# Four stacked graph-attention layers on one core: lighter VectorE work in the one-head layer, and the last layer's dense product turned round

## The chip, the cores and the metric

One core of a Trainium2 chip runs the whole program. The metric is device time in microseconds (us) of one launch; the time before is the median of three runs. A profiled execution of the same program gives the trace from which durations are read.

## The reference

Four graph-attention layers, each `x = x + gat(relu(layernorm(x)), adj)`, over 3327 nodes with 512 features in float32. The graph is sparse: a node has about 17 neighbours on average, itself among them. In each layer (heads 8, 4, 1, 8; head width 512 / heads):

```
h   = features @ W                                  # [n, heads, d]
e   = leaky_relu(s1[:, None] + s2[None, :], 0.2)    # s1, s2: one number per node and head
e   = where(adj > 0, e, -inf)
out = softmax(e, over neighbours) @ h               # layers 1 and 2 then take elu(out)
```

The slope is 0.2. A factor of `exp` that depends on the target node alone drops out of the softmax, which the kernel uses throughout.

## The kernel before

**Two ways to reach neighbours.** Nodes are sorted by neighbour count and cut into 26 tiles of 128 (`NT`), the fullest first. A tile's neighbours are listed in up to `CAPS[t]` slots per node (36, 25, 23, 22, ... 11). Most tiles go *by lists*: for each slot an indirect DMA, issued by POOL, gathers 128 rows of 528 floats (features and scores) from a table in DRAM. The first tiles are taken *dense* instead: 0, 1, 9 and 3 of them in layers 0 to 3 (`DENSE`). For these the 26 source tiles are walked in order, with a byte mask of who is whose neighbour.

**Steps.** A list tile works in groups of four slots. One group is a *step*: layer 2 (one head) has 72 steps, layer 3 (the last) has 105. A loop over steps writes the instructions of PE, DVE, ACT and POOL in an order fixed by hand. Within step `s` the order is: gathers for the step four ahead (`fetch`, five buffers, `LOOK = 5`; a list tile's own rows come by a DMA that SP issues), pieces placed "first", the next group's scores (`scored`), pieces placed "scored", this group's sums (`group`), pieces placed "last". Every other piece (dense work, ends of tiles) is put into this order with `later(s, place, piece)`. Each engine runs its instructions in this order and waits on semaphores.

**List groups.** `scored`: two DVE instructions form `z` (L888 adds target and source score, L890 is the leaky relu), ACT takes the exponential (L891); at a tile's first group DVE first copies the target's score out of the gathered row (L886). `group` with more than one head: DVE multiplies each gathered row by its weights (L919, `m`), PE adds the products into a PSUM bank with an identity matrix (L924, `bank<-m,ident`). With one head DVE does both in one instruction per slot (L912).

**End of a tile.** DVE divides by the sum of weights; then, except in the last layer, layer norm, four transposes (L451) and the 16-matmul projection to the next layer's table (L469).

**Dense tiles of layer 2 (`Wholes`).** Nine tiles in three passes of three. For source tile `j`: ACT makes the weights `r` of 128 sources x 384 targets in PSUM (`weights`, L1128), DVE adds `c` and applies the mask (`masked`, L1135, into `em`), PE multiplies (`products`, L1162, three matmuls 128 x 512). The sum of weights per target is built on the way: POOL adds `em` in pairs (`paired`, L1148), DVE adds two pairs and the running sum in a strided reduction (`added`, L1154), and at the end of a pass three small matmuls with a column of ones sum over partitions (`divisors`, L1169). `Whole.means` divides on DVE (L1089).

**Dense tiles of layers 1 and 3 (`Several`).** In layer 3, three tiles at once, in two passes of four heads. A *unit* is one source tile in one pass; there are 52. Per unit: two loads by SP (feature columns and mask, L1259 and L1260, three buffers each); ACT makes the weights of four heads (`weights`, L1276, 128 x 384 each) in three PSUM banks `r` and scales the features by `c` into `vs` (`features`, L1287, two buffers); one DVE instruction of 128 x 1536 masks all four heads (`masked`, L1292, into `e`, two buffers); and PE runs twelve matmuls (`products`, L1310), for each of three target tiles and four heads, with the 128 x 128 weights stationary and the head's 65 feature columns moving, each column run given twice, so 130 columns. Unit `u` stands in step `u * (steps - 8) / 52`; its products come one step later.

On this chip a float32 matmul shows as two records of the matmul and two of its weight load, so 624 of these matmuls are 1248 records.

Of the kernel before, what the change touches and what calls it, by code (L numbers as in the profile page):

```python
# [380 lines left out]
class Weights:  # L381
# [19 lines left out]
    def fold(self):  # L401

        if not self.left:
            return
        nc, HF = self.nc, self.HF
        s, k = self.left.pop(0)
        prod = self.work.tile([P, 2 * HF], F32, name="prod", bufs=1)
        nc.vector.tensor_mul(prod.rearrange("p (s n) -> p s n", s=2), self.w[:, k, :, :HF],
                             self.av[:, s, :].rearrange("p (s n) -> p s n", s=2))
        nc.vector.tensor_reduce(self.w[:, k, s, HF:HF + self.H],  # L410
                                prod.rearrange("p (h d) -> p h d", d=self.D), AX.X, OP.add)


# [383 lines left out]
def tile_gat_lists(ctx: ExitStack, tc: tile.TileContext, x, adj, ws, avs, out, ident, half, slots, L, low, spare, tabx, tabs):  # L797
# [48 lines left out]
    class Tile:  # L846
# [29 lines left out]
        def scored(self, i):  # L876

            H = HEADS[self.l]
            t = self.t
            k0, n, g = self.groups[i]  # L880
            if i == 0:
                self.po = pools["o"].tile([P, BANK], F32, name="bank")
                pw = next(scores)
                K = CAPS[t]
                self.wt, self.s = pw[:, :K * 8].rearrange("p (k h) -> p k h", h=8), pw[:, K * 8:K * 8 + H]
                nc.vector.tensor_copy(self.s, g[:, n, F:F + H] if self.l == 0 else g[:, 0, F // 2:F // 2 + H])  # L886
            z = small.tile([P, GROUP, 8], F32, name="z")[:, :n, :H]
            nc.vector.tensor_tensor(z, g[:, :n, ROW - 8:ROW - 8 + H],  # L888
                                    self.s.unsqueeze(1).to_broadcast([P, n, H]), OP.add)
            nc.vector.scalar_tensor_tensor(z, z, SLOPE, z, OP.mult, OP.max)  # L890
            nc.scalar.activation(self.wt[:, k0:k0 + n, :H], z, AF.Exp)  # L891
            if self.l == 0:
                ranks = n - (i == 0)
                nc.scalar.activation(slots(t, max(k0, 1), count=ranks), g[:, :ranks, F // 2], AF.Copy)
                if i == 0:
                    nc.scalar.activation(xs[self.t], g[:, n, :F], AF.Copy)
# [187 lines left out]
    class Whole(Tile):  # L1084


        def means(self):
            self.y = low[:, self.t % 3 * F:(self.t % 3 + 1) * F]
            nc.vector.tensor_scalar(self.y, self.po, self.den, None, OP.mult)  # L1089

    class Wholes:


        def __init__(self, l, W):
# [6 lines left out]
            self.a = [low[:, 5 * F + p % 2 * wide:5 * F + (p % 2 + 1) * wide] for p in range(ND // 3)]  # L1101
            self.v, self.e, self.mk, self.r, self.pairs, self.parts = {}, {}, {}, {}, {}, {}

# [14 lines left out]
        def weights(self, p, j):  # L1118
# [3 lines left out]
            if p == 0:  # L1122
# [3 lines left out]
                nc.scalar.activation(mc, c, AF.Copy, scale=-1.0)  # L1126
            r = self.r[p, j] = pools["o"].tile([P, wide], F32, name="r")
            nc.scalar.activation(r, self.a[p], AF.Relu, scale=b, bias=mc)  # L1128

        def masked(self, p, j):  # L1130

            if j % 2 == 0:
                self.two = pools["e"].tile([P, 2, wide], F32, name="em", bufs=3)
            self.e[p, j] = self.two[:, j % 2, :]
            nc.vector.scalar_tensor_tensor(self.e[p, j], self.r.pop((p, j)), self.c[:, j:j + 1],  # L1135
                                           self.mk.pop((p, j)), OP.add, OP.mult)
            if j % 2:
                self.pairs[p, j // 2] = self.two

        def part(self, p, i):  # L1140
            if (p, i) not in self.parts:
                self.parts[p, i] = pools["e"].tile([P, 3, wide], F32, name="parts", bufs=2)
            return self.parts[p, i]

        def paired(self, p, i):

            two = self.pairs.pop((p, i))
            nc.gpsimd.tensor_tensor(self.part(p, i // 2)[:, 1 + i % 2, :], two[:, 0, :], two[:, 1, :], OP.add)  # L1148

        def added(self, p, i):  # L1150

            parts = self.part(p, i // 2)[:, i < 2:2 + i % 2, :]
            out_ = self.a[p] if i == NT // 2 - 1 else self.part(p, i // 2 + 1)[:, 0, :]
            nc.vector.tensor_reduce(out_, parts.rearrange("p j c -> p c j"), AX.X, OP.add)  # L1154

# [9 lines left out]

        def divisors(self, p):
            self.pd = pools["t"].tile([P, F // P, P], F32, name="pt")
            for q in range(3):
                nc.tensor.matmul(self.pd[:, 0, q:q + 1], self.a[p][:, q * P:(q + 1) * P], one, start=True, stop=True)  # L1169

        def means(self, p):
            den = small.tile([P, 3], F32, name="den3")
            nc.vector.reciprocal(den, self.pd[:, 0, :3])
            for q in range(3):
                tl = self.tiles[3 * p + q]
                tl.den = den[:, q:q + 1]
                tl.means()

        def place(self, n):

            per = n // (ND // 3)
            for p in range(ND // 3):
                s0 = p * per
                later(s0 - 4 if p else -1, "first", lambda p=p: self.targets(p))
                for j in range(NT):
# [7 lines left out]
                    if j % 2:  # L1193
                        i = j // 2
                        later(s + 1, "first", lambda p=p, i=i: self.paired(p, i))
                        if i % 2 or j == NT - 1:
                            later(s + 2, "last", lambda p=p, i=i: self.added(p, i))
                later(s + 3, "first", lambda p=p: self.divisors(p))
                later(s + 3, "last", lambda p=p: self.means(p))
# [15 lines left out]
    class Several:  # L1215
# [3 lines left out]
        def __init__(self, l, n, W):  # L1219
# [11 lines left out]

            self.vs = [room((Q + (self.H == 8)) * DV) for _ in range(2)]
            self.v = [room(ROW // 2) for _ in range(3)]
            self.mk = [room(n * P // 4).bitcast(U8) for _ in range(3)]
            self.s = room(n * 8).rearrange("p (t h) -> p t h", h=8)
            for t in range(n):
                nc.sync.dma_start(self.s[:, t, :self.H],
                                  tabs[l % 2][t * P:(t + 1) * P, F // 2:F // 2 + self.H])
            self.per = BANK // DV - (self.H == 8)

        def begin(self):

            if self.H == 8:
                for vs in self.vs:
                    nc.scalar.activation(vs[:, self.Q * self.DV:], ident[:, :self.DV], AF.Copy, scale=0.0)
            for q in range(self.n):
# [48 lines left out]
        def products(self, u):  # L1295
# [8 lines left out]
            for q in range(self.n):  # L1304
                for h in range(Q):
                    o, o0 = self.where(q, h)
                    dst, mov = o[:, o0:o0 + DV], vs[:, h * DV:(h + 1) * DV]
                    if self.H == 8:
                        dst, mov = twice(dst, self.per * DV - o0), twice(mov, (Q - h) * DV)
                    nc.tensor.matmul(dst, e[:, h, q * P:(q + 1) * P], mov, start=False, stop=(j == NT - 1),  # L1310
                                     skip_group_check=True)

# [20 lines left out]
        def place(self, s0, s1):  # L1333
# [12 lines left out]
            for q in range(self.n):  # L1346
                self.tiles[q].ends(s + 1 + 2 * q)

    at = {}

# [10 lines left out]
    for l in range(NL):  # L1361
# [3 lines left out]
        with ExitStack() as c2:  # L1365
# [13 lines left out]
            else:  # L1379
                pools.update(m=pool("mpool", 5))  # L1380
                pools.update(p=pool("ps_p", 1 if DENSE[l] else 2, **psum))
                if DENSE[l]:
                    pools.update(w=pool("ps_w", l // 3 + 1, **psum), r=pool("ps_r", 1, **psum))
                    if DENSE[l] > 1:
                        pools.update(e=pool("epool", 1))
                    wholes = Several(l, DENSE[l], W)
                    pw = pools["p"].tile([P, BANK], F32, name="pw")
# [21 lines left out]
            elif DENSE[l]:  # L1409
                wholes.place(0, len(steps) - 8)  # L1410
            at_end = len(steps) + 30
# [69 lines left out]
```

## Time and profile before

| what | value |
|---|---|
| median of three runs | 2940.11 us (2933.88 to 2944.69) |
| profiled execution | 2959.5 us |
| its span, first to last instruction | 2957.8 us |
| mean granted TensorE clock | 0.867 |
| busy over the span | PE 75%, DVE 65%, POOL 58%, ACT 32% |
| DMA | 594.20 MB, 201 GB/s over the span |
| layer 2 in the trace | about 1856 to 2293 us |
| layer 3 in the trace | about 2300 to 2958 us |

The profile gives one execution. Busy time is the time in which an engine had an instruction running; a line such as L1310 names the kernel line. PE is the matmul, PEld its weight load. "Idle before, releaser" is how long an engine stood still ahead of these instructions and whose signal ended it; "issue" means that no signal is seen for which it waited.

### The profile page before, as it was taken

The page shows a single profiled execution, that of the slowest core. Times are in us where ns is not written, and L with a number is a line of the kernel's source. Part 1 is how long each engine was busy: PE and PEld are TensorE (multiplying, and loading weights), DVE is VectorE, ACT ScalarE, POOL GpSimd, SP SyncE. Part 2 cuts the span into 40 slices and gives each one's busy share as a digit, 9 for nine tenths or more (in the row PEclk, how much of TensorE's full clock was granted, in tenths as well). Part 3 has the DMA queues.
Part 4 walks back from the last instruction along what each step waited for, and adds up shares of the span by engine and source line. Part 5 has one row for each costly group of instructions (what it writes and reads, how often), then busy time and mean ns, then how long its engine had stood idle before and what let it go on. Part 6 is the DMA issues. An engine that isn't in the chain of part 4 may idle for free.

```text
span 2957.8 us, 27080 instructions
## 1 busy us (share of the span) xinstructions
PE 2224.7 (75%) x7082; PEld 1251.4 (42%) x7082; DVE 1914.3 (65%) x4968; ACT 931.8 (32%) x2502; POOL 1728.5 (58%) x1717
## 2 busy tenths in 40 slices
PE   4777677787677745788877787689696778877887
PEld 2664243343333323344434344245354445444453
DVE  7887656565546523767765565698887556666665
ACT  5882122222221101323332222344333333333330
POOL 7894465565556663555655552676764555555554
PEclk9988788888888877899988889799897889988898
DMA  6885477677666675666766663788775666666664
GB/s 229 322 294 160 140 218 216 193 235 222 188 205 195 189 194 170 181 202 192 209 193 189 192 192 111 226 264 257 236 248 152 191 177 184 185 182 194 185 187 137
DMA packets 260730, 594.20 MB, mean 201 GB/s; under 512 B 103699, under 2 KB 121107, under 8 KB 256214
## 3 DMA queue, kind: packets, MB, share of 16 engines
q0 software_dynamic: 124368, 432.13, 49.8%
q1 hardware_dynamic: 132454, 153.45, 16.5%
q10 hardware_dynamic: 3744, 6.82, 0.7%
q8 instruction: 57, 0.93, 0.1%
q14 instruction: 107, 0.88, 0.1%
HBM read 542.60 MB, written 49.65 MB: 200 GB/s over the span
## 4 chain that ended last, share of the span: by engine, by line
DVE 21%; PE 18%; issue 16%; another core or an unknown queue 11%; ACT 6%; POOL 4%; DMA 3%; DVEq 0%; ACTq 0%; POOLq 0%; SPq 0%
PE bank L924 11%; DVE m L919 9%; POOL g L835 3%; PE pv L469 3%; PE whole L1310 3%; DVE bank L912 2%; DMA g<-tab,idxb 1%; DVE z L890 1%; DVE z L888 1%; ACT r L1276 1%; DVE x L962 1%; DVE q L439 1%; ACT pw L891 1%; DVE room L1292 1%
## 5 line engine op out<-in xcount | busy, mean ns | idle before, releaser
L924 PE MATMUL bank<-m,ident 128*128 128x512 f32 x2414 | 1236.5, 659 | 268.9 <-DVE m L919 137.5
L835 POOL DMA_INDIRECT g<-tab,idxb x712 | 678.2, 952 | 465.5 <-issue 189.3
L919 DVE TENSOR_TENSOR m<-g,pw 128x512 f32<-128x512 f32 x1207 | 752.0, 682 | 267.6 <-ACT pw L891 193.5
L924 PEld LDWEIGHTS bank<-m,ident 128*128 128x128 f32 x2414 | 490.2, 211 | 879.8 <-issue 568.9
L469 PE MATMUL pv<-w,hT 128*128 128x264 f32 x1664 | 447.4, 423 | 107.0 <-ACT hT L458 71.2
L835 POOL DMA_INDIRECT g<-tabx,twiceb x342 | 324.1, 948 | 245.8 <-issue 124.4
L835 POOL DMA_INDIRECT g<-tab,idxa x297 | 283.1, 953 | 262.1 <-DMA tab<-v 88.5
L469 PEld LDWEIGHTS pv<-w,hT 128*128 128x128 f32 x1664 | 339.5, 208 | 215.2 <-ACT hT L458 79.6
L891 ACT ACTIVATE pw<-z 128x32 f32<-128x32 f32 (+4 forms) x356 | 67.8, 190 | 945.4 <-DVE z L890 509.8
L1162 PE MATMUL whole<-ve,em 128*128 128x512 f32 x468 | 224.5, 632 | 48.2 <-DVE em L1135 27.9
L1310 PE MATMUL whole<-L,room 128*128 128x130 f32 x1248 | 171.1, 288 | 79.2 <-issue 79.0
L1310 PEld LDWEIGHTS whole<-L,room 128*128 128x128 f32 x1248 | 163.1, 201 | 107.1 <-issue 104.7
L695 POOL TENSOR_TENSOR key<-a,keys 128x3328 int32<-128x3328 int32 (+1 forms) x29 | 189.5, 6539 | 15.9 <-DVE cand L704 12.6
L912 DVE SCALAR_TENSOR_TENSOR bank<-g,L,bank 128x512 f32<-128x512 f32 x243 | 183.3, 754 | 9.9 <-remote 2.0
L835 POOL DMA_INDIRECT g<-tabx,twicea x99 | 94.4, 954 | 119.6 <-issue 75.3
L1162 PEld LDWEIGHTS whole<-ve,em 128*128 128x128 f32 x468 | 92.8, 203 | 158.7 <-issue 114.6
L451 PE MATMUL pt<-ident,xn 128*128 128x128 f32 x416 | 74.5, 302 | 93.0 <-issue 32.2
L704 DVE MAX8 cand<-key 128x8 f32<-128x208 int32 x416 | 143.6, 363 | 0.1
L890 DVE SCALAR_TENSOR_TENSOR z<-z 128x32 f32<-128x32 f32 (+5 forms) x428 | 82.5, 193 | 91.4 <-remote 61.4
L919 DVE TENSOR_TENSOR bank<-g,pw 128x512 f32<-128x512 f32 x74 | 51.5, 696 | 126.7 <-ACT pw L891 105.6
L1276 ACT ACTIVATE r<-low,L 128x384 f32<-128x384 f32 x208 | 121.2, 582 | 9.8 <-remote 3.9
L888 DVE TENSOR_TENSOR z<-g,pw 128x32 f32<-128x32 f32 (+4 forms) x356 | 61.8, 174 | 94.9 <-DMA g<-tab,idxa 39.0
(181 smaller groups left out, 2154.4 us busy)
## 6 DMA issues: line engine op xcount, KB each, us to landing
a<-in_adj SPq DMA_DIRECT2D x25, 1664.0 KB
tab<-v SPq DMA_DIRECT2D x78, 264.0 KB
ve<-tab SPq DMA_DIRECT2D x78, 264.0 KB
g<-tab SPq DMA_DIRECT2D x65, 264.0 KB
tabx<-vx SPq DMA_DIRECT2D x26, 528.0 KB
g<-tab,idxb POOLq DMA_INDIRECT x712
low<-tab SPq DMA_DIRECT2D x52, 132.0 KB
spare<-tab SPq DMA_DIRECT2D x52, 132.0 KB
```

The costliest lines, as they stand in the source:

```text
L469: nc.tensor.matmul(pv[:, s, :HF + 8], hT[:, k, :], W.w[:, k, s, :], start=(k == 0), stop=(k == KC - 1))
L695: nc.gpsimd.tensor_tensor(key[:, c:c + quarter], a[:, c:c + quarter], keys[:, c:c + quarter], OP.mult)
L704: nc.vector.max(cand[:, g * 8:(g + 1) * 8], key[:, g * SEG:(g + 1) * SEG])
L835: nc.gpsimd.indirect_dma_start(out=out_, out_offset=None, in_=table, in_offset=bass.IndirectOffsetOnAxis(ap=which, axis=0))
L890: nc.vector.scalar_tensor_tensor(z, z, SLOPE, z, OP.mult, OP.max)
L891: nc.scalar.activation(self.wt[:, k0:k0 + n, :H], z, AF.Exp)
L912: nc.vector.scalar_tensor_tensor(acc, v, w, acc, OP.mult, OP.add)
L919: nc.vector.tensor_tensor(out_.rearrange("p (s h d) -> p s h d", s=2, d=D), v.rearrange("p s (h d) -> p s h d", d=D), wt[:, k0 + q, :H].re ...
L924: nc.tensor.matmul(self.po, ident, m[:, q, :], start=False, stop=(k0 + q == K - 1), skip_group_check=True)
L1162: nc.tensor.matmul(tl.po.rearrange("p (s m) -> p s m", s=2), e[:, q * P:(q + 1) * P], v.rearrange("p (s m) -> p s m", s=2)[:, :, :F // 2], ...
L1276: nc.scalar.activation(self.r[:, h, :], self.a[:, g, :], AF.Relu, bias=-1.0, scale=self.b[:, j, g:g + 1])
L1310: nc.tensor.matmul(dst, e[:, h, q * P:(q + 1) * P], mov, start=False, stop=(j == NT - 1), skip_group_check=True)
```

## The change

In the one-head layer, the table of features carries two more columns: 0.8 times the target's score and 0.2 times the source's. The score `z` becomes `max(s2 + 0.8 s1, 0.2 s2)`, one DVE instruction, and ACT copies the target's score. `Whole.means` goes to ACT. The weights `r` get one PSUM bank for the whole layer, and the sums of weights go into columns of the same bank: POOL's pair sums are summed over partitions by PE, three matmuls of one column for each pair of source tiles, in place of the DVE reductions.

In the last layer `Turned` takes the place of `Several`: four passes of two heads, 104 units. The 65 feature columns of a head are stationary, and its weights for all three target tiles (384 columns) move: two matmuls per unit. Results stand transposed, so each pass ends with copies out of PSUM, 24 PE transposes in all for the four passes, and the division. Per unit the mask is 128 x 768, `vs` has three buffers, `e` two, and each unit has its own load of mask and features. Units are spread over half steps ("first" and "last"), with three steps between passes. Layer 1 keeps `Several`, whose eight-head branches go.

```diff
@@ Weights.fold
+        if self.H == 1:
+            nc.vector.tensor_scalar(self.w[:, k, s, HF + 1:HF + 2], self.w[:, k, s, HF:HF + 1],
+                                    SLOPE if s else 1.0 - SLOPE, None, OP.mult)
@@ Tile.scored
-                nc.vector.tensor_copy(self.s, g[:, n, F:F + H] if self.l == 0 else g[:, 0, F // 2:F // 2 + H])
+                if H == 1:
+                    nc.scalar.activation(self.s, g[:, 0, F // 2 + 1:F // 2 + 2], AF.Copy)
+                else:
+                    nc.vector.tensor_copy(self.s, g[:, n, F:F + H] if self.l == 0 else g[:, 0, F // 2:F // 2 + H])
             z = small.tile([P, GROUP, 8], F32, name="z")[:, :n, :H]
+            if H == 1:
+                nc.vector.scalar_tensor_tensor(z, g[:, :n, ROW - 8:ROW - 7], self.s, g[:, :n, ROW - 7:ROW - 6],
+                                               OP.add, OP.max)
+                nc.scalar.activation(self.wt[:, k0:k0 + n, :H], z, AF.Exp)
+                return
@@ Whole.means
-            nc.vector.tensor_scalar(self.y, self.po, self.den, None, OP.mult)
+            nc.scalar.activation(self.y, self.po, AF.Copy, scale=self.den)
@@ Wholes
+            bank = pools["o"].tile([P, BANK], F32, name="r")
+            self.r, self.pd = bank[:, :wide], [bank[:, wide + 8 * p:wide + 8 * p + 3] for p in range(ND // 3)]
...
         def paired(self, p, i):
             two = self.pairs.pop((p, i))
-            nc.gpsimd.tensor_tensor(self.part(p, i // 2)[:, 1 + i % 2, :], two[:, 0, :], two[:, 1, :], OP.add)
+            self.sums[p, i] = pools["e"].tile([P, wide], F32, name="sums", bufs=3)
+            nc.gpsimd.tensor_tensor(self.sums[p, i], two[:, 0, :], two[:, 1, :], OP.add)
         def added(self, p, i):
-            parts = self.part(p, i // 2)[:, i < 2:2 + i % 2, :]
-            out_ = self.a[p] if i == NT // 2 - 1 else self.part(p, i // 2 + 1)[:, 0, :]
-            nc.vector.tensor_reduce(out_, parts.rearrange("p j c -> p c j"), AX.X, OP.add)
+            both = self.sums.pop((p, i))
+            for q in range(3):
+                nc.tensor.matmul(self.pd[p][:, q:q + 1], both[:, q * P:(q + 1) * P], one, start=(i == 0 and q == 0),
+                                 stop=(i == NT // 2 - 1), skip_group_check=True)
...
-                        if i % 2 or j == NT - 1:
-                            later(s + 2, "last", lambda p=p, i=i: self.added(p, i))
-                later(s + 3, "first", lambda p=p: self.divisors(p))
+                        later(s + 3, "first", lambda p=p, i=i: self.added(p, i))
@@ Turned (new; takes Several's place in layer 3)
+        def features(self, u):
...
+            for h in range(Q):
+                nc.scalar.activation(vs[:, h, :D], self.v[u % 3][:, h * D:(h + 1) * D], AF.Copy,
+                                     scale=self.c[:, j, h0 + h:h0 + h + 1])
+            nc.scalar.activation(vs[:, :, D], self.c[:, j, h0:h0 + Q], AF.Copy)
+        def masked(self, u):
+            n = self.n * P
+            nc.vector.scalar_tensor_tensor(self.e[u % 2], self.r, 1.0,
+                                           self.mk[u % 3].unsqueeze(1).to_broadcast([P, self.Q, n]), OP.add, OP.mult)
+        def products(self, u):
+            j, e, vs, DV = u % NT, self.e[u % 2], self.vs[u % 3], self.DV
...
+            for h, o in enumerate(self.po):
+                nc.tensor.matmul(o[:DV, :self.n * P], vs[:, h * DV:(h + 1) * DV], e[:, h, :], start=(j == 0),
+                                 stop=(j == NT - 1))
...
+        def turned(self):
...
+                    nc.tensor.transpose(self.pt[:, q, h, :], self.sums[:DV, h, q * P:(q + 1) * P], ident[:DV, :DV])
...
+            halves = 2 * (s1 - s0 - 3 * (self.passes - 1))
+            for u in range(self.passes * NT):
+                i, j = divmod(u, NT)
+                s, b = divmod(2 * (s0 + 3 * i) + u * halves // (self.passes * NT), 2)
+                place = "last" if b else "first"
+                later(s, place, lambda u=u: self.masked(u))
+                later(s, "last" if b else "scored",
+                      lambda u=u: (self.weights(u + 1), self.features(u + 1), self.load(u + 3)))
+                later(s + 1, place, lambda u=u: self.products(u))
+                if j == NT - 1:
+                    later(s + 2, "scored", self.summed)
+                    later(s + 3, "first", self.turned)
+                    later(s + 3, "last", lambda i=i: self.means(i))
@@ tile_gat_lists
-                wholes.place(0, len(steps) - 8)
+                wholes.place(0, len(steps) - (10 if many else 8))
```

## The prediction

> **What bounds the kernel now.** First the busy time by stage: the window view over layer 2's dense part and over layer 3 (columns: window, length, busy time and records of PE, PEld, DVE, ACT, POOL, granted clock, DMA share, GB/s).
>
> ```profile
> 1856.00:2230.00 374.00, 308.29 (x891) 168.32 (x892) 313.75 (x630) 146.53 (x361) 257.48 (x273) 0.91 0.80 244
> 2300.00:2950.00 650.00, 521.34 (x2001) 308.45 (x2000) 408.39 (x800) 202.66 (x629) 362.66 (x382) 0.89 0.64 183
> ```
>
> Layer 2: DVE 84%, PE 82%, POOL 69%. But each gather is followed by 0.30 us of issue, so POOL's 215 gathers in this window hold it 215 x (0.97 + 0.30) = 273 us, with pair sums (38) and roots (13) 324: three engines close to full. Layer 3: PE 80%, DVE 63%, POOL with 383 x 0.30 of issue about 478 of 650.
>
> Next, what DVE does in these stages that the change touches (groups by line and form: busy us, mean ns | idle before). The first four lines are of 1856 to 2293 us, the last two of the whole page:
>
> ```profile
> L1154 DVE TENSOR_REDUCE parts<-parts 128x384 f32<-128x1152 f32 x15 | 22.0, 1467 | 0.0
> L890 DVE SCALAR_TENSOR_TENSOR z<-z 128x4 f32<-128x4 f32 x58 | 14.2, 245 | 4.3 <-DVE z L888 2.4
> L1089 DVE TENSOR_SCALAR low<-whole,den 128x512 f32<-128x512 f32 x9 | 6.2, 744 | 0.1
> L1135 DVE SCALAR_TENSOR_TENSOR em<-r,c,mk 128x384 f32<-128x384 f32 x78 | 47.8, 612 | 24.8 <-issue 10.1 <-ACT r L1128 8.5 <-ACT hT L458 4.8
> ...
> L924 PE MATMUL bank<-m,ident 128*128 128x512 f32 x2414 | 1236.5, 659 | 268.9 <-DVE m L919 137.5
> L1310 PE MATMUL whole<-L,room 128*128 128x130 f32 x1248 | 171.1, 288 | 79.2 <-issue 79.0
> ```
>
> The last line is odd: 79 us of idle ahead of products that wait for no signal. The timeline shows what it is. These lines are from one spot of layer 3 (start, length, engine, instruction, idle before):
>
> ```profile
> 2415.71 2.17 PE L1310 MATMUL whole<-L,room 128*128 128x130 f32 x18
> ...
> 2418.78 0.27 PE L1310 MATMUL whole<-L,room 128*128 128x130 f32 x1 [0.89 <-issue]
> ...
> 2420.18 0.19 PEld L1310 LDWEIGHTS whole<-L,room 128*128 128x128 f32 x1 [2.37 <-issue]
> 2420.84 0.94 POOL L835 DMA_INDIRECT g<-tab,idxa  x1 [0.30 <-issue]
> 2421.59 0.38 PE L1310 MATMUL whole<-L,room 128*128 128x130 f32 x1 [2.54 <-issue]
> ...
> 2425.85 0.95 POOL L835 DMA_INDIRECT g<-tab,idxa  x1 [0.30 <-issue]
> 2426.50 0.38 PE L1310 MATMUL whole<-L,room 128*128 128x130 f32 x1 [1.75 <-issue]
> ...
> 2430.30 1.06 ACT L1287 ACTIVATE L<-spare,low 128x64 f32<-128x64 f32 x4 [8.51 <-remote]
> ...
> 2431.57 2.48 DVE L919 TENSOR_TENSOR m<-g,pw 128x512 f32<-128x512 f32 x4 [9.54 <-ACT pw L891]
> ```
>
> PE runs 18 of this unit's 24 product records in 2.17 us; the last six take 12 us, one instruction per 0.7 or 1.4 us. ACT waits for them (it may not overwrite `vs`), its exponential comes late, and DVE stands 9.54 us. I call this a slow stretch. Searching the trace for PE starts 0.7 or 1.4 us apart without a wait gives 15 in layer 3 with 106 us together (which fits the idle <-issue in layer 3: 79.0 before L1310 and 26.6 before L924), 10 in layer 1 with 55, and none in layer 2. Nearly all begin 11 to 23 us into an unbroken run of POOL gathers, when PE has run 100 to 135 instructions since the run began (in layer 1 some earlier, from 60), and end 0 to 7 us after it. Layer 2's runs are broken by POOL's pair sums and roots. What holds PE there the trace does not say; when it comes is what I use.
>
> So layer 3 is PE's: 521 us busy and 106 us slow stretches are 627 of 650. At full clock its instructions need less: L924 720 records x 0.43 us (spacing of back-to-back records) = 310, L1310 1248 x 0.112 (24 in 2.68 us) = 140, with 8 of other matmuls 458; the other 63 go to half clock, which the records grant for 3.4 to 13.7 us after most slow stretches.
>
> **Base.** The profiled execution took 2959.5 us (span 2957.8 and 1.7 around it), 19.4 above the median 2940.1. I add up the change against the profile and take it off the median.
>
> **Layer 2, DVE.** Gone: the reductions, 22.0 + 2.9 + 2.9 (the two shorter forms, three each at 0.96) = 27.8 us; one of two `z` instructions, 14.2 + 2.3 of smaller groups = 16.5; the nine means 6.2; 16 score copies 2.3. Sum 52.8 of the stage's 314. New: eight one-column multiplications in `fold`, 8 x 0.15 (as L964's one-column row) = 1.2 us, in earlier layers.
>
> **Layer 2, PE.** 117 matmuls of one column for nine of the old kind, 108 more, each two loads and two matmuls. Price between 2 x 0.112 (L1310's spacing) and 2 x 0.20 (the old nine, L1169: 18 records, 3.6 us): 24 to 43 us, and I take 24, since most would run at full clock. PE gets to 332 of 374, so it is late next, with POOL at 324. DVE's 53 us therefore cannot be had in full: with a dozen us of waits the floor is about 344.
>
> **Layer 2, a new wait.** `r` and the sums share a bank, and the instruction order of the changed kernel shows what follows: each group of three sum matmuls waits for ACT's last write of `r` and for POOL's pair sum, and the next `masked` on DVE waits for these matmuls. They stand first in PE's step, so 39 times DVE must wait until PE has finished its previous step. Before, DVE could run several units ahead. Behind `masked` on DVE stand the scores and four L912 (3.1 us) of the step, and for them wait gather buffers and so POOL. A PE step with a projection holds 16 records x 0.224 = 3.6 us of L469, 0.6 of transposes and 2.6 of products. The wait costs between 0 (DVE at 4.1 us a step is now the faster one and PE never starves) and 39 x 2.6 = 101 us (a whole unit of products each time); I take 10, because PE is the slower engine in either case and DVE's waiting then costs only where steps are uneven. ACT's score copy now stands ahead of DVE's `z`, queued behind `r`: 16 x 0 to 16 x 0.9 us, 5. Means on ACT (39% busy): hidden. So of the 53, PE's and POOL's floor leaves 374 - 344 = 30, and 30 - 10 - 5 = 15 us gained, between a loss of 85 (30 - 101 - 14) and a gain of 35.
>
> The Trainium skill (PSUM — Partial Sum Buffer, section "PSUM bank collisions raise a hardware error") asks that engines be kept apart by bank and not by address. That rule speaks against putting sums beside `r`; the price of keeping apart is the wait above, and the sum is the same without it.
>
> **Layer 3, PE.** 208 matmuls of 384 columns: 416 records x 0.32 (three quarters of 0.43) = 133 us for 140, and 24 small transposes 24 x 0.3 = 7 at most. Streaming time does not move. What moves is the count: records of L924 and products together fall from 720 + 1248 = 1968 to 720 + 416 = 1136, and with as many weight loads from 10.9 to 6.3 per gather. 100 to 135 instructions are then reached after some 19 gathers (24 us) instead of 11, as in layer 1, which has (1420 + 1420) / 406 = 7.0 per gather and spends 55 / 643 = 8.6% in slow stretches. 8.6% of about 580 is 50, for 106 now: 56 us gained, and with it a somewhat smaller share, 25, of the 63 at half clock. Bounds: 0 and 106 + 50.
>
> **Layer 3, DVE, ACT, DMA.** `masked`: 0.95 us per unit by interpolation between 1.745 (1536 elements) and 0.416 (256), 104 x 0.95 = 99 for 91: 8 us more, beside PE. ACT: 52 more of L1288 (0.19), eight copies (0.58): 15 us on an engine 31% busy. SP issues 104 more loads (0.32 each); the loads now land 1.5 to 4.5 us after issue by the packet records, and are asked for two units, 10 us, ahead: hidden.
>
> **Layer 3, a tighter wait.** `e` has two buffers of half the work, so `masked(u)` waits for `products(u-2)`, which the order puts half a step to a step before it; now it is two or three steps. Where the unit stands "first" and its forerunner's products "last" in the step before (about 36 of 104 units), PE has nothing left while DVE does `masked` (0.95), `z` (0.4) and the first `m` (0.68): 2.2 us of PE idle with signals, in half of them only 0.95, as another product follows. At most 18 x 2.2 + 18 x 0.95 = 57, at least 0; I take 25. Layer 3: 56 + 25 - 25 = 56, and 7 of streaming less 7 of transposes. I take 58, between -57 and the 136 that POOL's pace allows (below).
>
> **Sum.** 15 + 58 - 1 = 72: 2940 - 72 = 2868 us.
>
> The Trainium skill (TensorE: Matmul & The Clock Gate, section "HAM oscillation — how this bites in real kernels") says that idle gaps of PE over some 3.4 us bring its clock to half. The trace agrees: windows of 3.4 us at half clock, and 0.78 granted from 900 to 1162 us, where PE is 64% busy. It speaks against a change that leaves PE less to do: at 0.78 layer 3's 458 us would take 587, and nearly all of the 58 would be gone.
>
> **Rivals.** *Slow stretches stay* (0.2): they depend on gathers, not on PE's count. For: run lengths set their end. Against: runs of 20 to 38 gathers without a slow stretch stand in the trace, with few PE instructions for each gather. Then layer 3 gains 0 to 10, all in all 2910 to 2950, say 2925. *Both layers reach POOL's pace* (0.12): layer 3 falls from 6.1 us a step to 4.7, 97 x 1.4 = 136, layer 2 gains 35: 2770. *The shared bank decides* (0.18, the slower side): DVE waits in layer 2 for most of a projection step, 39 x 4.2 = 164 us, less the 53 saved, a loss of 111, against 58 in layer 3: 2993. It ends slower than before once the wait costs over 53 + 58 = 111 us, 2.8 us each time. For: PE and DVE are level in layer 2 and PE's projections come in lumps. Against: PE can go on with products while DVE is late.
>
> **Numbers.** The forecast has 0.5. Its own range is 2800 to 2910. To hold 0.8 the range takes that, the first rival, half of the second and the nearer part of the slower one (0.06): 2790 to 2965. Half a per cent, 14.7 us, is about what a measurement of this kernel can tell from no change. Faster: 0.5 + 0.12 + half of the first rival = 0.72; same 0.1; slower 0.18.
>
> **What would show it.** Right: L1154 gone, DVE in layer 2 near 260 us; in layer 3 slow stretches of about 50 us and PE's "issue" idle halved. Wrong: DVE idle over 100 us ahead of `em` with PE as releaser; PE idle in layer 3 behind DVE's `m` instead of "issue"; a granted clock under 0.8 there.

## The result: slower by 2.7 %

The changed kernel took 3020.61 us (median of four runs, 3019.61 to 3023.30), the kernel before 2942.40 us beside it: a ratio of 1.0271, with an interval from 1.0232 to 1.0310. That is 78 us more where the prediction had 72 us less, and above its range (2790 to 2965). The profiled execution took 3023.3 us (span 3021.6).

First the window view over the dense products of layer 2 and of layer 3 (columns as in the prediction's first fence), of the kernel before and then of the kernel after:

```profile
1859.00:2231.00 372.00, 309.19 (x892) 168.39 (x892) 313.76 (x630) 145.19 (x355) 255.94 (x270) 0.91 0.80 244
...
2322.00:2912.00 590.00, 481.28 (x1913) 290.33 (x1912) 375.54 (x728) 191.29 (x594) 330.37 (x349) 0.90 0.65 185
```

```profile
1846.00:2238.00 392.00, 339.63 (x1108) 195.42 (x1107) 275.17 (x530) 152.95 (x377) 256.62 (x270) 0.92 0.76 230
...
2324.00:2971.00 647.00, 472.46 (x1083) 190.41 (x1082) 380.72 (x776) 199.22 (x656) 327.13 (x345) 0.89 0.59 171
```

In layer 2 DVE's work has indeed fallen, from 313.76 us to 275.17, and still the stretch takes 392 us instead of 372. In layer 3 PE has no more to do than before (472 us for 481), its records have fallen by 43 % (1913 to 1083), and the stretch takes 647 us instead of 590. Together that is 77 us, about what the medians differ by.

Where the time of layer 3 went is in the groups by line and form. The first line is of the kernel before (2300 to 2958 us), the others of the kernel after (2300 to 3021 us); behind the second bar stands the idle time ahead of the group and what ended it:

```profile
L924 PE MATMUL bank<-m,ident 128*128 128x512 f32 x720 | 358.1, 645 | 46.1 <-issue 26.6 <-DVE m L919 19.3
```

```profile
L936 PE MATMUL bank<-m,ident 128*128 128x512 f32 x720 | 372.2, 662 | 176.5 <-DVE m L931 155.5 <-issue 14.5 <-DVE z L902 5.8
...
L1424 DVE SCALAR_TENSOR_TENSOR L<-r,room 128x768 f32<-128x768 f32 x52 | 49.6, 953 | 89.6 <-PE whole L1433 30.7 <-remote 26.2 <-issue 15.7
L1424 DVE SCALAR_TENSOR_TENSOR spare<-r,room 128x768 f32<-128x768 f32 x52 | 49.5, 953 | 94.8 <-issue 40.5 <-remote 38.3 <-PE whole L1433 8.8
```

PE's wait for DVE's `m` has grown from 19.3 to 155.5 us, and DVE now stands 184 us ahead of `masked` (L1424), for 39 us ahead of the old L1292 before (the expectations below count 174). The two engines wait for each other in turn. The timeline of one spot shows how:

```profile
2509.54 1.88 DVE L931 TENSOR_TENSOR m<-g,pw 128x512 f32<-128x512 f32 x3 [0.27 <-ACT pw L903]
...
2510.28 5.16 PE L936 MATMUL bank<-m,ident 128*128 128x512 f32 x6 [5.19 <-DVE m L931]
...
2515.28 1.45 PE L1433 MATMUL whole<-spare,room 128*65 128x384 f32 x4
...
2516.83 0.96 DVE L1424 SCALAR_TENSOR_TENSOR spare<-r,room 128x768 f32<-128x768 f32 x1 [4.70 <-PE whole L1433]
...
2519.71 2.84 PE L936 MATMUL bank<-m,ident 128*128 128x512 f32 x6 [1.69 <-DVE m L931]
...
2521.12 0.94 POOL L838 DMA_INDIRECT g<-tab,idxb  x1 [5.97 <-DVE m L931]
```

PE has stood 5.19 us for DVE's `m`. It does the bank matmuls of the step first and the products on `spare` last. DVE needs that buffer for its next `masked` and stands 4.70 us until these products are done. Then PE has nothing until DVE has made the next `m`, and POOL's gathers wait for the buffers that `m` frees. The standing has a second price: the granted clock was a half from 2508.2 to 2515.0 us by the trace's clock records, and the six matmuls after the wait take 5.16 us, the next six 2.84.

### The profile page after: what moved, and what is told of

It is laid out like the page before. It is cut to its first block, busy times and chain, and to the rows that moved or that the text cites. A ratio compares the mean times of both kernels' runs of the same rounds, so it can differ in the third digit from the quotient of the medians.

```text
span 3021.6 us, 26325 instructions
## 1 busy us (share of the span) xinstructions
PE 2241.4 (74%) x6482; PEld 1176.0 (39%) x6482; DVE 1876.7 (62%) x4909; ACT 946.2 (31%) x2586; POOL 1731.4 (57%) x1717
## 5 line engine op out<-in xcount | busy, mean ns | idle before, releaser
L936 PE MATMUL bank<-m,ident 128*128 128x512 f32 x2414 | 1251.3, 664 | 397.0 <-DVE m L931 272.7
L1173 PE MATMUL whole<-ve,em 128*128 128x512 f32 x468 | 233.8, 650 | 20.4 <-issue 9.8
L902 DVE SCALAR_TENSOR_TENSOR z<-z 128x32 f32<-128x32 f32 (+4 forms) x356 | 65.7, 185 | 85.7 <-remote 45.8
L479 ACT ACTIVATE v<-pv,root 128x528 f32<-128x528 f32 x78 | 53.8, 690 | 193.0 <-remote 96.4
L1424 DVE SCALAR_TENSOR_TENSOR spare<-r,room 128x768 f32<-128x768 f32 x52 | 49.5, 953 | 94.8 <-issue 40.5
```

The source lines that it names most:

```text
L936: nc.tensor.matmul(self.po, ident, m[:, q, :], start=False, stop=(k0 + q == K - 1), skip_group_check=True)
L1173: nc.tensor.matmul(tl.po.rearrange("p (s m) -> p s m", s=2), e[:, q * P:(q + 1) * P], v.rearrange("p (s m) -> p s m", s=2)[:, :, :F // 2], ...
```

## The experiments

All are compared with the kernel before on the same chip, since the chips that took part fall into two kinds, a sixth apart: on kind S (one chip) the kernel before took 2949 and 2952 us, like the first measurement, on kind F (two chips, the second for t1 and t2) 2442, 2441 and 2439. "Products" is the time from the first to the last product matmul of the layer in the profiled execution; for the old layer 3 it begins with the matmuls that zero the banks, 2 us earlier (before, in the first measurement: 372 and 590 us).

| run | kind | median us | ratio to before (interval) | products layer 2, layer 3 |
|---|---|---|---|---|
| changed kernel, first measurement | like S | 3020.6 | 1.0271 (1.0232 to 1.0310) | 392, 646 |
| e1_layer2 | S | 2967.6 | 1.0068 (1.0044 to 1.0092) | 398, 586 |
| e2_layer3 | S | 2994.1 | 1.0176 (1.0118 to 1.0234) | 372, 644 |
| e3_three_e | S | 2960.4 | 1.0033 (0.9994 to 1.0071) | 392, 574 |
| e4_four_e | S | 2947.8 | 0.9999 (0.9967 to 1.0031) | 390, 567 |
| s1_r_in_sbuf | S | 2914.5 | 0.9872 (0.9834 to 0.9911) | 370, 564 |
| s2_sums_on_dve | S | 2926.4 | 0.9917 (0.9884 to 0.9951) | 368, 574 |
| s3_runs_broken | S | 2938.3 | 0.9941 (0.9915 to 0.9967) | 371, 583 |
| s4_all_broken | S | 2922.6 | 0.9899 (0.9835 to 0.9963) | 367, 571 |
| r1_after (changed kernel) | F | 2548.3 | 1.0432 (1.0414 to 1.0451) | 369, 544 |
| e5_r_in_sbuf, again as r2_r_in_sbuf | F | 2446.8, 2447.2 | 1.0021, 1.0020 (1.0005 to 1.0034) | 353, 455 |
| e6_sums_on_dve, again as r3_sums_on_dve | F | 2449.0, 2449.3 | 1.0031, 1.0030 (1.0015 to 1.0046) | 352, 455 |
| e7_layer3_four_e | F | 2452.5 | 1.0047 (1.0032 to 1.0062) | 356, 455 |
| e8_r_sbuf_copy_dve | F | 2449.0 | 1.0021 (1.0006 to 1.0035) | 358, 455 |
| r4_runs_broken | F | 2453.7 | 1.0049 (1.0031 to 1.0067) | 358, 445 |
| t1_products_early | F | 2463.5 | 1.0084 (1.0052 to 1.0116) | 368, 456 |
| t2_early_r_in_sbuf | F | 2445.0 | 1.0020 (1.0004 to 1.0036) | 353, 456 |

### Which layer

One kernel has the changed layer 2 and the old `Several` in layer 3, the other the old layer 2 and `Turned`.

```
e1:  ...
     -                    wholes = (Turned if many else Several)(l, DENSE[l], W)
     +                    wholes = Several(l, DENSE[l], W)
e2:  class Whole, class Wholes, Tile.scored and Weights.fold as in the kernel before
```

> The changed layer 2 alone (one z instruction, score copy and means on ACT, row sums as matmuls in r's bank), layer 3 as before (Several). Theory T (the loss is made in layer 3 by the two half-size e buffers: masked(u) on DVE must wait until PE has done products(u-2), which PE starts only after the bank matmuls of a whole step): layer 2 moves little, so 2930 to 2960 us against 2942 of the kernel before, the dense products of layer 2 lasting within 15 us of the 371 us of before. Rival S (the shared bank in layer 2 decides): 2980 us or more, with DVE idle over 50 us ahead of the masked instructions of layer 2 and PE's sum matmuls as releaser.

> The changed layer 3 alone (Turned), layer 2 as before. Theory T: it carries the whole loss, 3000 to 3020 us against 2942 (some 60 to 75 us more in layer 3), with 150 to 200 us of DVE idle ahead of the masked instructions and slow stretches of PE under 20 us. Rival S (layer 2's shared bank makes the loss): 2930 to 2960 us.

Both layers lose, and the losses nearly add: 0.68 % and 1.76 %, for 2.71 % together. Layer 3 makes about two thirds of it (644 us of products for 590). Theory T, which gave layer 3 the whole, missed both times: 2994 us for 3000 to 3020, and 2968 for 2930 to 2960, with 26 us more in layer 2's products and not "within 15". Rival S missed too (2980 or more, and PE's sum matmuls as the main releaser: they ended 19 us of DVE's waits ahead of `masked` there).

### Layer 3: buffers

```
-            self.e = [room(self.Q * wide).rearrange("p (h c) -> p h c", h=self.Q) for _ in range(2)]
+            self.e = [room(self.Q * wide).rearrange("p (h c) -> p h c", h=self.Q) for _ in range(3)]
...          self.e[u % 2] becomes self.e[u % 3]; the room tile has 10 banks instead of 8
e4:          four e and four vs buffers, 12 banks
```

> The changed kernel with three e buffers in Turned instead of two (a larger room tile), so that masked(u) waits for products(u-3). Theory T: DVE's idle ahead of masked falls from 174 us to under 80, PE's idle ahead of the bank matmuls from some 160 us to under 90, and the time from 3020 to 2900 to 2965 us. Rival O (the order of work is the cause: products stand behind the bank matmuls in PE's queue, r has one buffer, and the half steps make PE and DVE wait for each other whatever the buffers): the idle moves from masked to the next instruction on DVE or to ACT, and the time stays within 1% of 3020 us (2990 to 3040). Of the slow stretches of PE: if they follow from unbroken runs of gathers, they come back (over 40 us) once DVE no longer breaks the runs; if from PE's instruction count per gather, they stay under 30 us.

> The changed kernel with four e and four vs buffers in Turned. Theory T: as with three e buffers, or up to 30 us less (2880 to 2960 us), since then neither masked nor the feature copies wait for the products of the step before. Rival O: within 1% of 3020 us.

Nothing but buffers changed, and the products of layer 3 fell from 646 to 574 and 567 us, the whole from 1.027 to 1.003 and 1.000. Rival O, which expected the time to stay, is out. DVE's idle ahead of `masked` fell from 184 us to 38 with three buffers, but it is 76 with four; PE's wait for `m` fell from 155.5 us to 87 and 77, so only about half of it went with the buffers. What holds the engines in the other half is taken up below. On kind F, the runs r1_after and r2_r_in_sbuf have the same layer 3 but for two or four buffers, and its products took 544 and 455 us. The window view of these stretches, r1_after first:

```profile
1961.00:2505.00 544.00, 454.43 (x1081) 182.53 (x1080) 379.48 (x775) 198.16 (x649) 329.20 (x348) 0.96 0.71 204
```

```profile
1949.00:2403.00 454.00, 424.64 (x1080) 178.77 (x1079) 377.77 (x776) 198.77 (x651) 328.71 (x347) 0.99 0.84 244
```

The whole kernel lost 4.3 % on kind F (r1_after), more than the 1 to 3 % that T gave it there.

### Layer 3: place

With the buffers shown to matter, it was open whether an earlier place of PE's products would do as well as more buffers. These runs, on kind F alone, leave the two buffers and move the products half a step forward, ahead of the bank matmuls:

```
-                later(s + 1, place, lambda u=u: self.products(u))
+                later(*((s + 1, "first") if b else (s, "scored")), lambda u=u: self.products(u))
```

> The changed kernel, still with two e buffers, but with each unit's products on PE half a step earlier: products of a unit masked at the head of a step stand ahead of that step's bank matmuls, those of a unit masked at its end at the head of the next step. Theory T2 (masked(u) waits because products(u-2) stand behind the bank matmuls, which wait for DVE's m): the idle of DVE ahead of masked falls from 174 us to under 70 and layer 3 gets most of the gain that four buffers gave: within 25 us of the kernel with four e buffers, that is 2935 to 2975 us where before takes some 2945, and 2460 to 2490 us where before takes 2442. Rival W (with the products early PE waits for masked instead, before each step's bank matmuls): within 1% of the changed kernel, 3000 to 3040 or 2530 to 2560 us.

> The same with r of layer 2 in SBUF: the changed kernel with two edits and no more buffers in layer 3. Theories T2 and B: 15 to 35 us less than without the second edit, so 2905 to 2950 us where before takes some 2945, level with four buffers and r in SBUF (0.987 of the kernel before), and 2445 to 2465 us where before takes 2442. Rival W: 2970 to 3010 or 2515 to 2545 us.

Groups of layer 3 on kind F: first the changed kernel (r1_after, 1940 to 2552 us), then with the products early (t1, 1940 to 2465 us).

```profile
L936 PE MATMUL bank<-m,ident 128*128 128x512 f32 x720 | 355.6, 637 | 102.7 <-DVE m L931 102.5
L1424 DVE SCALAR_TENSOR_TENSOR L<-r,room 128x768 f32<-128x768 f32 x52 | 49.6, 954 | 55.3 <-PE whole L1433 33.2 <-issue 8.4 <-ACT spare L1420 6.7
L1424 DVE SCALAR_TENSOR_TENSOR spare<-r,room 128x768 f32<-128x768 f32 x52 | 49.6, 954 | 48.7 <-issue 32.9 <-PE whole L1433 9.8 <-ACT spare L1420 4.7
```

```profile
L936 PE MATMUL bank<-m,ident 128*128 128x512 f32 x720 | 333.7, 604 | 26.6 <-DVE m L931 26.4
L1424 DVE SCALAR_TENSOR_TENSOR spare<-r,room 128x768 f32<-128x768 f32 x52 | 49.5, 953 | 5.3 <-ACT r L1408 5.3
L1424 DVE SCALAR_TENSOR_TENSOR L<-r,room 128x768 f32<-128x768 f32 x52 | 49.5, 952 | 11.4 <-ACT r L1408 11.4
```

PE no longer ends any of DVE's waits ahead of `masked` (104 us of idle fall to 17), PE's own wait for `m` falls from 102.5 to 26.4 us, and the products take 456 us: the gain of four buffers, without one more byte. So two buffers are enough there when the products that free them do not stand behind the bank matmuls of a whole step. Rival W is out. t2, with the second edit below, is level with four buffers and r in SBUF (both 1.002). On kind S the early place was not run.

### Layer 2

Four kernels, all with four e and vs buffers in layer 3:

```
e5, s1:  -            self.r, self.pd = bank[:, :wide], [bank[:, wide + 8 * p:wide + 8 * p + 3] for ...]
         +            self.r = pools["e"].tile([P, wide], F32, name="rs", bufs=1)
         +            self.pd = [bank[:, wide + 8 * p:wide + 8 * p + 3] for ...]
e6, s2:  row sums as in the kernel before (pair sums on POOL, reductions on DVE)
e7:      the whole of layer 2 as in the kernel before
e8:      e5, and the score copy as nc.vector.tensor_copy
```

> The kernel with four e and four vs buffers, and in layer 2 r in SBUF (one buffer, as before) instead of in the bank of the row sums; the sums stay matmuls. So masked waits no more for PE's sum matmuls, nor these for ACT's r. Base: four e buffers ran 2948 us, its layer 2 products last 390 us (372 before). Theory B (the shared bank makes layer 2 longer): the products of layer 2 take 360 to 375 us, DVE idle ahead of masked falls from 74 us to under 35, and the time is 2920 to 2935 us. Rival P (the 234 extra records in PE's queue make it longer): products 385 to 395 us and 2940 to 2955 us.

> The kernel with four e and four vs buffers, and in layer 2 the row sums on DVE again as in the kernel before (pair sums on POOL, reductions on DVE, r in its own bank); the single z instruction, the score copy and the means on ACT stay as changed. Theory B and rival P both expect the loss of layer 2 gone: products 360 to 375 us, 2920 to 2940 us. Rival Z (the score copy queued on ACT behind r, which z then waits for, makes layer 2 longer): products 385 us or more, 2940 to 2955 us.

> Layer 2 as before the change, layer 3 changed with four e and four vs buffers. If the effects of the layers add (layer 2 changed alone cost 0.7%, and both together with four e buffers were level with before), 0.993 of the kernel before: 2920 to 2935 us. If layer 3 gains nothing with four buffers, 2940 to 2955 us.

> As the kernel with four e and four vs buffers and r in SBUF, and besides the score copy of layer 2 back on DVE. Rival Z: 5 to 20 us less than with the copy on ACT, the 20 us of DVE idle ahead of z gone. Theory B: within 5 us of the kernel with r in SBUF.

These four ran on kind F, where the times expected for kind S have no meaning and only ratios and products can be read. Two of them ran again there, beside the changed kernel itself:

> The changed kernel itself beside the others, since the kernel before took 2949 us on one chip and 2442 us on another, where its gathers run unbroken and PE shows no slow stretches. On a chip of the first kind: 1.02 to 1.03 of the kernel before. On the other: theory T (two e buffers make PE and DVE wait for each other) still expects a loss, 1.01 to 1.03; if POOL's gathers alone set the pace there, 1.00 to 1.005.

> Four e and four vs buffers, r of layer 2 in SBUF; on the faster chip this ran 1.002 of the kernel before. On a chip where before takes some 2940 us, theory B (shared bank) expects the products of layer 2 to take 360 to 375 us (390 with the shared bank) and 0.990 to 0.996 of the kernel before; rival P (extra matmuls in PE's queue) 385 to 395 us and 0.997 to 1.003.

> Four e and four vs buffers, row sums of layer 2 on DVE as before, z, score copy and means as changed. On a chip where before takes some 2940 us: theory B and rival P 360 to 375 us for the products of layer 2 and 0.990 to 0.996 of the kernel before; rival Z (the score copy on ACT) 385 us or more and 0.997 to 1.003.

And the same two kernels on kind S:

> Four e and four vs buffers, r of layer 2 in SBUF. On the faster chip: 1.002 of the kernel before, as twice already. On a chip where before takes some 2940 us: theory B (shared bank) 360 to 375 us for the products of layer 2 (390 with the shared bank) and 0.990 to 0.996 of the kernel before; rival P (extra matmuls in PE's queue) 385 to 395 us and 0.997 to 1.003.

> Four e and four vs buffers, row sums of layer 2 on DVE, the rest of the change kept. On a chip where before takes some 2940 us: theory B and rival P 360 to 375 us for the products of layer 2; rival Z (score copy on ACT) 385 us or more.

Groups of layer 2: the changed kernel (1846 to 2238 us), then s1 (1843 to 2214 us), where all lines stand one lower:

```profile
L1149 DVE SCALAR_TENSOR_TENSOR em<-r,c,mk 128x384 f32<-128x384 f32 x77 | 47.3, 615 | 71.5 <-PE r L1164 25.2 <-ACT r L1142 15.8 <-remote 14.3
L1164 PE MATMUL r<-one,sums 128*128 128x1 f32 x228 | 31.6, 254 | 32.2 <-ACT L L898 16.4 <-ACT L L890 8.0 <-POOL sums L1158 3.8
```

```profile
L1150 DVE SCALAR_TENSOR_TENSOR em<-rs,c,mk 128x384 f32<-128x384 f32 x78 | 62.1, 796 | 30.4 <-issue 19.2 <-ACT rs L1143 6.9 <-POOL root L434 3.4
L1165 PE MATMUL r<-one,sums 128*128 128x1 f32 x228 | 29.4, 244 | 12.4 <-issue 7.7 <-POOL sums L1159 4.7
```

With the same matmuls on PE, but r out of their bank, DVE's idle ahead of `masked` falls from 71.5 to 30.4 us and PE no longer ends any of it. The products take 370 us instead of 390, and the whole gains 1.3 % over e4 (ratio 0.9872 for 0.9999). On kind F it is the same: 353 us for the 369 of r1_after. So it is the shared bank (theory B), not the number of matmuls (rival P). The score copy on ACT (rival Z) costs nothing: s2, which keeps it there, takes 368 us on kind S, and on kind F e8, with the copy on DVE, has the ratio of e5.

What the saved DVE work itself brings is small. With the wait gone layer 2's products take 370 us on S; the kernel before has 372. On kind F it is 353 against 356 for the old layer 2 (e7). In s1 DVE is busy 291 us of this stretch for 314 before: 39 us saved, less 15 that `masked` takes longer with r in SBUF (last section). So 23 us of DVE's work bought 2 to 3 us.

s1, the changed kernel with more buffers in layer 3 and r out of the shared bank, is the fastest version run on kind S: 37 us faster than the kernel before (2951.7 to 2914.5), 1.3 %, an interval clear of 1. Some 28 us of that lie in the products of the two layers (370 for 372, 564 for 590); where the rest lies is not shown. On kind F none beats the kernel before.

### The slow stretches

A last pair asked whether long runs of gathers make PE's slow stretches, by a small POOL addition after every second group of gathers, in the kernel before and in s1:

```
+            if i % 2:
+                nc.gpsimd.tensor_tensor(tick, tick, tick, OP.add)
```

> The kernel before with one small addition on POOL (8 columns, about 0.5 us) after every second group of gathers, so that no run of gathers is longer than about 8. Theory G (PE's slow stretches come from long unbroken runs of POOL gathers, and layer 2 has none because its pair sums break the runs): on a chip where before takes some 2940 us, slow stretches fall from 225 us to under 60 and the time falls by 2 to 8%. Rival N (the breaks do not matter, the stretches follow from how many instructions PE executes): slow stretches stay over 150 us and the time rises by 0 to 3%. On a chip with 2442 us: 1 to 4% slower, since POOL's gathers set the pace there.

> The kernel before with a small addition on POOL after every second group of gathers. On a chip where before takes some 2940 us: theory G (long runs of gathers hold back PE's semaphore events) expects the times without such events to fall from 821 us to under 300 and the time to fall by 2 to 8%; rival N (a break of 0.5 us is too short, or the runs are not the cause) no fall, 0 to 3% slower. On the faster chip 1.005, as before.

> Four e and four vs buffers, r of layer 2 in SBUF, and the small additions on POOL. On a chip where before takes some 2940 us: theory G 0.92 to 0.98 of the kernel before, rival N 0.99 to 1.03. On the faster chip 1.005 to 1.010.

On kind S the slow stretches stayed (180 to 220 us in the whole execution, depending on how they are counted; 225 before), and s4 is no faster than s1. The 0.6 % that s3 gained is unexplained. Theory G is not borne out, at least for breaks this short. On kind F r4 lost 0.5 %, half of the least that was expected (1 to 4 %).

## Why the prediction was wrong

In layer 3 the prediction had 58 us less (its own terms, 56 + 25 - 25, give 56) and 57 us more were measured. Two of its terms make that difference, in about equal parts.

**The first step that failed: "Layer 3, a tighter wait."** The mechanism was right, and the count too: 36 units were named, and on kind F DVE waited 33 times for over 1 us and went on 0.09 us after the products of two units before had ended (99 us together, of 101 in waits over 1 us). The size was wrong: taken at 25 us with a bound of 57, it cost 79 us on kind S (products 646 us, 567 with four buffers) and 89 on kind F (544 and 455). On kind F, where no other wait of PE shows in this stretch, the two rows above say what it is made of. PE's idle time falls from 90 to 29 us, 60 us; so the idle alone came to a little more than the bound, which priced half of the units at 0.95 us. And PE's busy time falls from 454 to 425 us for the same work, as the granted clock rises from 0.96 to 0.99 (48 us at half clock with two buffers, 7 with four): 30 us that the term put at nothing, since it did not ask what the waits do to the clock.

On kind S not all waiting is of this kind. Of the 35 waits of DVE over 1 us ahead of `masked` that do not end with ACT's `r`, 21 (85 us) ended 0.09 us after the products of two units before; the other 14 (85 us) ended 1.8 to 12.3 us after them. These 14 look like what the next step describes.

**The second step that failed: "Layer 3, PE."** As predicted, slow stretches of PE went with its record count, and further: 106 us before, 7 after, 3.5 with four buffers. But the 56 us that this was to bring did not come. In the products of layer 3 PE was idle for 109 us of 590 before; with four buffers it is idle for 110 of 567 (window view of e4_four_e):

```profile
2329.00:2896.00 567.00, 456.52 (x1081) 190.60 (x1080) 381.93 (x782) 201.45 (x658) 329.36 (x348) 0.91 0.69 196
```

The idle time has only changed its name, from "issue" to DVE's `m` (19 us before, 77 now, for the whole of layer 3). All of the 23 us that are gained is busy time of PE, 481 to 457 us, near the 25 that the prediction expected from the clock; whether the clock made them is not shown (granted 0.90 and 0.91). At the following spot, with four buffers on kind S, PE shows no slow stretch, and DVE and ACT stand instead:

```profile
2524.34 1.45 PE L1433 MATMUL whole<-room 128*65 128x384 f32 x4
...
2525.53 0.94 POOL L838 DMA_INDIRECT g<-tab,idxb  x1 [0.30 <-issue]
2529.86 0.59 ACT L1418 ACTIVATE room<-room,low 128x64 f32<-128x64 f32 x2 [9.75 <-remote]
2529.96 0.96 DVE L1424 SCALAR_TENSOR_TENSOR room<-r,room 128x768 f32<-128x768 f32 x1 [8.45 <-issue]
```

Four engines are still for 3.4 us after the last gather. The trace's semaphore events say what they wait for: nine matmuls that signal end from 2518.88 to 2525.79 us, and of PE's signals none is recorded from 2518.43 to 2529.07; then sixteen come within 1.4 us, most of them 42 ns apart, and ACT and DVE go on. Set beside the same layer on kind F (r2), DVE falls behind at 19 places, by 2 to 11 us each, 110 us together, which is nearly all that the products of layer 3 take longer (567 us for 455). At 11 of the 19 (72 us) a burst of six or more signals of PE comes at most 1.2 us before DVE goes on; kind F has no such burst. At the other 8 nothing of the kind shows. So two thirds of what e4 loses there against kind F go with late signals. That PE's slow stretches in the kernel before are the same thing, seen on another engine, fits, but is not shown.

What the turned product is worth without them is seen on kind F, where there are no such stretches: nothing. e7, with layer 3 alone changed and four buffers, is 0.5 % slower than the kernel before, and its products take 455 us where the old ones in r4 take 445, POOL's additions included. On kind S it is worth some 20 us by the medians of e1 (old layer 3) and e4, 2967.6 and 2947.8; from the end of layer 2's products to the end of the profiled runs it is 12 (718.5 and 706 us).

**"Layer 2, a new wait."** Taken at 10 us, it costs 16 (F) to 20 (S). Here the mechanism was right and the size somewhat off, and the rival that had it at 164 us was far too high: DVE was released late by PE in 10 places with 25 us together, not 39 times by 4.2. That rival held the whole of the 0.18 given to "slower"; the kernel came out slower mainly for another reason.

**"PE's and POOL's floor leaves 30."** The floor was set at 344 us, and without the wait 370 (S) and 353 (F) were measured. So the 30 us were 2 to 3. On F PE is busy for 324 of the 353 us: there PE is the bound the prediction named, with 29 us of waits for the dozen it allowed. What adds 17 us on S is not told apart; late signals may be part of it.

**Right** were the prices read from rows: `masked` at 0.95 us, and PE's added work in layer 2 (some 30 us, forecast 24, at most 43). DVE in layer 2 was forecast near 260 us and has 275, in part because the single `z` instruction takes 0.33 us where each of the two took 0.25. The sign named as wrong, "PE idle in layer 3 behind DVE's `m` instead of issue", is what the trace shows. The clock of 0.78 that was feared for layer 3 did not come (0.89; 0.90 before).

## What to carry to other kernels

When a change halves a buffer, look at what stands between the two users of it on the engine that frees it: a release that is queued behind a whole step's work makes two engines take turns. Price such a wait for every unit that meets it, and ask what the standing does to the clock (60 and 30 us here, for 25 in the forecast). The first cure to try is an earlier place for the releasing instruction, which on kind F did as much as two more buffers, and only then more buffers. Idle time that goes from one engine need not leave the kernel: look for where the trace puts it next. Work taken off an engine that is not alone at the limit buys little (23 us for 2 to 3), and a shared PSUM bank can cost more than that (16 to 20 us).

## What the runs showed of the hardware

The kernel before took 2949 us on one chip and 2442 on another. Two kernels that are alike up to layer 2 (e4 on S, e5 on F) run within 3 us of each other up to the time when the gathers of layer 0 begin (some 275 us); from there to 710 us S falls behind in jumps of up to 12 us, by 100 us in all. Gathers take the same 0.95 us and land as fast (median 3.5 us after issue on S and 3.7 on F, by the packet records). On F the gathers of the changed kernel run unbroken for up to 408 us (327 of them) with no slow stretch in that time, so long runs alone do not make them. What differs is the signals: on S each profiled execution has 95 to 115 stretches of over 3 us in which four or more signalling matmuls of PE end and no signal is recorded, 1.0 to 1.2 ms together; on F none has any. Not every such stretch need be a late signal, because on S a fifth to a quarter of PE's signals have no record at all (1444 events for 1876 signalling matmuls in e4; on F all have one). The waits that end at a burst, counted above, are the better evidence. What delays the signals was not found.

With r in SBUF, 15 of the 78 `masked` of s1 took 0.86 to 2.11 us instead of 0.62. Each of the 15 overlaps one of POOL's pair sums; with r in PSUM, 13 overlapped one and all took 0.62. The Trainium skill (SBUF — State Buffer, section "SBUF: two separate sides") says that a VectorE operation with two SBUF inputs and a GpSimd operation that reads SBUF lock each other out of a port for a whole instruction; the runs agree in 15 of the 16 cases of s1 in which the two overlapped, and the price was 15 us of DVE's time, which did not keep the products from falling to 370 us.
